# A ternary feed-forward laid between the steps of the next batch's attention

## The chip, the cores and the metric

The kernel runs on one NeuronCore of a Trainium2 chip. The metric is the device time of one execution in microseconds, the median of several runs. The profile is of one further execution. The engines are called by their short names: PE (TensorE, with PEld for its weight loads), DVE (VectorE), ACT (ScalarE), POOL (GpSimd) and SP (SyncE, which here only issues DMAs).

## The reference, cut to what matters

Eight sequences of 512 tokens and 128 features go through two transformer blocks with adaptive layer norm (shift, scale and gate come from a small conditioning vector). The first block has a one-head attention and a feed-forward with 4-bit quantization; nothing of it changes. The second block has an attention with 16 heads of 8 features, whose logits get a bias from "read" and "write" lines, and a feed-forward with ternary weights. It is this feed-forward that the change moves:

```
h  = layernorm(x) * (1 + scale) + shift
g  = silu(h @ w1.T * s1) * (h @ w2.T * s2)        # 128 -> 512
g  = gelu(g @ h1.T * t1)                          # 512 -> 512, ternary weights
g  = gelu(g @ h2.T * t2)                          # 512 -> 512
x  = x + gate * (g @ w3.T * s3)                   # 512 -> 128
```

The attention of a batch needs nothing of another batch, and so does the feed-forward of a batch: the second only needs the first of the same batch.

## The kernel before, in words

All of x stays in SBUF (`X`, 128 tokens by 32 tiles by 128). A batch is four tiles of 128 tokens. Everything is float32. The stages follow each other over all eight batches: first block's attention, first block's feed-forward, second block's attention (`attention1`), second block's feed-forward (the loop at the end).

The second attention is written out by hand (`tc.manual_schedule()`): the order of the calls is the order in each engine's queue. Its unit is a group of four heads of one batch, 32 groups in all. A group goes through three units of query tiles (`UNITS`: tiles 0 and 1 together, tile 2, tile 3) in four steps:

- `scores1` (L605): PE makes the scores of four heads in two pairs of PSUM banks (`quad`).
- `softmax1` (L622, L626, L629, L633): for each pair DVE adds the bias and takes the maximum, ACT takes the exponential.
- `turn1` (L646) and `turned1` (L652): PE transposes the probabilities of one head into a bank with tag "tp", of which there are two, and ACT copies them to SBUF.
- `values1` (L663): PE multiplies them with v and sums in a bank with tag "acc".
- `prep1` (L553 to L572) prepares queries and keys of the next group, and `lines1` (L584 to L594) its bias, into the same pairs of banks as the scores.
- `outcome1` (L676 to L699) takes a group's sums, divides and, after the fourth group of a batch, applies the output projection `py` and adds it to X. It is a generator: each `go(ended)` runs one more piece, between the steps of the next group.
- `front1` is a generator, too: norm, projections, lines and their norm for the next batch, one piece after each step (`go(front)`). Its logarithm and exponential at L528 and L531 stand on ACT.

The pools: eight PSUM banks are two "tp", two "acc" and four in the pairs. Tiles of queries' packs and keys' packs are kept twice (`packs["q", b % 2]`).

The last stage, the feed-forward, works on four batches at a time. It first makes w1 and w2 products (L794, L795), silu on 512 columns with the scale in the activation (L797) and the product (L798) for all four; then for each batch the two hidden layers (L814, 32 products, gelu L818 on 512 columns), the last layer (L825), the addition to X (L829) and the output DMA (L830). It has four PSUM banks ("mm") in turn besides the two "acc".

Of the kernel before, what the change touches and what calls it, by code (L numbers as in the profile page):

```python
# [10 lines left out]
F32 = mybir.dt.float32  # L11
# [6 lines left out]
P = 128  # L18
# [14 lines left out]
def kernel(ctx: ExitStack, tc: tile.TileContext, a: dict, out: bass.AP):  # L33
# [21 lines left out]
    def acc(name):  # L55
        return ps.tile([P, 512], F32, tag="acc", bufs=2, name=name)
# [338 lines left out]
    def lines_setup(pool):  # L395
# [48 lines left out]
        packs = {}  # L444
        for i in range(2):
            for name in ("q", "k"):
                pk = pool.tile(
                    [P, NT, H, 32], F32, tag=f"pack_{name}{i}", bufs=1, name=f"pack_{name}{i}"
                )
                nc.gpsimd.memset(pk, 0.0)  # L450
                packs[name, i] = pk
            pk = pool.tile([P, NT, H * VW + 32 - VW], F32, tag=f"pack_v{i}", bufs=1, name=f"pack_v{i}")
            nc.gpsimd.memset(pk, 1.0)
            packs["v", i] = pk
# [4 lines left out]

    def front1(pool, st, b, stats, bqs, packs):  # L460

        xb = X[:, b * NT : (b + 1) * NT, :]
        qp, kp, vp = (packs[name, b % 2] for name in "qkv")
# [18 lines left out]
        for t in range(NT):  # L482
            cur = hT[:, 1 + t * P : 1 + (t + 1) * P]
            pb = acc(f"pb_{b}_{t}")
# [20 lines left out]
        nc.gpsimd.tensor_sub(ln, ln, m2)  # L505
        for t in range(NT):
            cur = hT[:, 1 + t * P : 1 + (t + 1) * P]
            pa = acc(f"pa_{b}_{t}")
# [11 lines left out]
            if t == 1:  # L520
                nc.scalar.activation(m2, ln, AF.Square)
                ss = pool.tile([P, nln], F32, tag="ss", bufs=1, name=f"ss_{b}")
                nc.vector.tensor_reduce(ss, m2, AX.X, ALU.add)
                nc.vector.tensor_scalar_max(ss, ss, 1e-24)
            yield

        lg = pool.tile([P, nln], F32, tag="lg", bufs=1, name=f"lg_{b}")
        nc.scalar.activation(lg, ss, AF.Ln)  # L528
        rn = pool.tile([P, NT, 2, H], F32, tag="rn", bufs=1, name=f"rn_{b}")
        rv = rn.rearrange("p t w h -> p (t w h)")  # L530
        nc.scalar.activation(rv, lg, AF.Exp, scale=-0.5)  # L531
        nc.gpsimd.tensor_mul(lg, rv, rv)
        nc.gpsimd.tensor_mul(lg, lg, ss)
        nc.gpsimd.tensor_scalar(lg, lg, -0.5, 1.5, ALU.mult, ALU.add)
        nc.gpsimd.tensor_mul(rv, rv, lg)
        nc.gpsimd.tensor_mul(
            rn[:, :, 1, :], rn[:, :, 1, :], bsc.unsqueeze(1).to_broadcast([P, NT, H])
        )
        yield
        lnv = ln.rearrange("p (t w h) e -> p t w h e", t=NT, w=2)  # L540
        over = lambda w: rn[:, :, w, :].unsqueeze(3).to_broadcast([P, NT, H, NL])
        nc.gpsimd.tensor_mul(kp[:, :, :, 0:NL], lnv[:, :, 0], over(0))

        nc.gpsimd.tensor_mul(qp[:, :, :, 0:NL], lnv[:, :, 1, :, ::-1], over(1))
        yield

    def prep1(pool, st, b, g, packs, dk, dq):

        qp, kp = packs["q", b % 2], packs["k", b % 2]
# [7 lines left out]
        qT = pool.tile([P, T], F32, tag="qT", name=f"q1T_{b}_{g}")  # L557
        nc.scalar.copy(qT, pq)  # L558
        kT = pool.tile([P, T], F32, tag="kT", name=f"k1T_{b}_{g}")
# [15 lines left out]
    def lines1(pool, st, b, g, wdiag):  # L575
# [12 lines left out]
        st["bias", b, g] = bias = pool.tile([P, 4, NT, P], F32, tag="bias", name=f"bias_{b}_{g}")  # L588
# [61 lines left out]
    def turned1(st, b, g, u, j):  # L650
        pT, pt = st["pT", b, g, u, j]
        nc.scalar.copy(pT[:, : width1(u)], pt[:, : width1(u)])  # L652

    def values1(st, b, g, u, packs):

        if u == 0:
            st["po", b, g] = acc(f"po1_{b}_{g}")
# [12 lines left out]
    def outcome1(pool, st, b, g):  # L670
# [16 lines left out]
        if g == NG - 1:  # L687
# [5 lines left out]
            py = acc(f"py1_{b}")  # L693
# [6 lines left out]
            yield  # L700

    def attention1(pool, stats, dk, dq, wdiag, bqs, packs):
# [6 lines left out]
        go = lambda gen: next(gen, None)  # L709
        first = front1(pool, st, 0, stats, bqs, packs)  # L710
        for _ in first:
            pass
# [3 lines left out]
        for at, (b, g) in enumerate(groups):  # L716
            before = groups[at - 1] if at else None
            after = groups[at + 1] if at + 1 < len(groups) else None
            if g == 0:
                for _ in front:  # L720
                    pass
# [178 lines left out]
```

## Time and profile before

| | |
|---|---|
| median of 3 runs | 1687.32 us (1686.17 to 1698.59) |
| the profiled execution | 1685.65 us, span of its instructions 1683.6 us |
| mean granted clock of PE | 0.803 |
| PE busy | 1317.8 us, 78% |
| DVE, ACT, POOL busy | 753.9, 719.1 and 428.5 us |
| second attention | 485 to 1363 us |
| second feed-forward | 1363 us to the end |

The times count from the first instruction. A busy time of PE says how long matmuls were in flight; the granted clock says how fast they ran. The two have to be read together: the same matmul takes twice as long at clock 0.5. A window is a stretch of the span with the busy time of each engine in it. "Lxxx" is a line of the kernel before.

### The profile page before, as it was taken

The numbers are of one execution on the slowest core, as the hardware profiler recorded it, in microseconds if no ns is written. First come the engines' busy times: TensorE is split into PE (matmuls) and PEld (weight loads), VectorE is DVE, ScalarE is ACT, GpSimd is POOL, SyncE is SP. The second block draws the span as 40 slices with busy tenths as digits, with TensorE's granted clock in tenths as the row PEclk, the third lists the DMA queues.
The fourth block names the chain that finished last, engine by engine and source line by source line (L and its number), as shares of the span: only waits on it lengthen the run. The fifth ranks groups of instructions, "written<-read, shape, count | busy, mean of one in ns | idle before, by whom it ended". The sixth has DMA issues, their size and how long they took to land.

```text
span 1683.6 us, 22090 instructions
## 1 busy us (share of the span) xinstructions
PE 1317.8 (78%) x8644; PEld 814.0 (48%) x8644; DVE 753.9 (45%) x1545; ACT 719.1 (43%) x1440; POOL 428.5 (25%) x524
## 2 busy tenths in 40 slices
PE   4699343553448888988888888888888889999999
PEld 4355132433335555555555555555555544444444
DVE  3866854454425555455555555455545541003000
ACT  3243211221346555655555665555556552114111
POOL 0210322111254424343343244342432200000000
PEclk9799677676757777677687877777777789999999
DMA  6000000000000000000000000000000000000000
GB/s 178 1 1 0 1 0 0 0 0 0 0 0 1 1 1 1 1 1 1 1 1 1 2 1 1 1 1 1 1 1 2 1 1 1 13 7 7 7 7 12
DMA packets 14317, 10.96 MB, mean 7 GB/s; under 512 B 1862, under 2 KB 12678, under 8 KB 14214
## 3 DMA queue, kind: packets, MB, share of 16 engines
q1 hardware_dynamic: 12054, 8.02, 1.6%
q10 hardware_dynamic: 2160, 1.54, 0.3%
q8 instruction: 68, 1.11, 0.3%
q14 instruction: 35, 0.29, 0.1%
HBM read 7.46 MB, written 2.10 MB: 6 GB/s over the span
## 4 chain that ended last, share of the span: by engine, by line
PE 52%; ACT 13%; DVE 4%; POOL 2%; issue 2%; ACTq 0%; POOLq 0%; DVEq 0%
PE ph L814 13%; PE pr1T L646 11%; PE s L605 9%; ACT pr L633 7%; PE po L663 4%; ACT p1T L652 2%; PE pi L584 2%; PE ogT L159 2%; PE pg L794 2%; PE py L825 2%; PE pu L795 2%; DVE nm L629 1%; PE pa L509 1%; ACT k1T L560 1%; PE py L695 1%
## 5 line engine op out<-in xcount | busy, mean ns | idle before, releaser
L652 ACT COPY p1T<-pr1T 128x384 f32<-128x384 f32 (+1 forms) x384 | 195.7, 522 | 247.7 <-PE pr1T L646 247.4
L646 PE MATMUL pr1T<-ident,pr 128*128 128x128 f32 x1280 | 273.0, 369 | 23.7 <-ACT p1T L652 16.9
L605 PE MATMUL s<-kd,qd 14*128 14x128 f32 (+3 forms) x1024 | 196.5, 600 | 80.2 <-ACT pr L633 62.1
L646 PEld LDWEIGHTS pr1T<-ident,pr 128*128 128x128 f32 x1280 | 198.8, 187 | 110.8 <-ACT p1T L652 49.9
L633 ACT ACTIVATE pr<-s,nm 128x128 f32<-128x128 f32 (+3 forms) x512 | 234.6, 547 | 3.0 <-DVE nm L629 2.9
L814 PE MATMUL ph<-g,c_h 128*128 128x512 f32 x512 | 222.0, 592 | 0.0
L629 DVE TENSOR_REDUCE nm<-s 128x2 f32<-128x256 f32 (+3 forms) x256 | 205.0, 821 | 6.6
L814 PEld LDWEIGHTS ph<-g,c_h 128*128 128x128 f32 x512 | 96.4, 190 | 116.7 <-issue 116.7
L605 PEld LDWEIGHTS s<-kd,qd 14*128 14x128 f32 x1024 | 69.7, 224 | 154.4 <-ACT pr L633 69.9
L594 POOL TENSOR_SCALAR_AFFINE_SELECT bias<-bias 128x512 f32<-128x512 f32 x128 | 77.1, 635 | 208.2 <-DVE bias L590 208.2
L818 ACT ACTIVATE g<-ph,c_scl 128x512 f32<-128x512 f32 x64 | 44.0, 688 | 196.3 <-PE ph L814 196.3
L590 DVE TENSOR_TENSOR bias<-pi,wdiag 128x512 f32<-128x512 f32 x128 | 79.4, 683 | 104.3 <-PE pi L584 104.3
L357 PE MATMUL yTp<-ident,q_xn_y 128*88 128x128 f32 x128 | 27.5, 388 | 117.3 <-DVE q_xn_y L252 117.3
L829 DVE TENSOR_TENSOR X<-X,py 128x512 f32<-128x512 f32 x8 | 5.5, 687 | 243.3 <-PE py L825 243.3
L663 PE MATMUL po<-p1T,pack_v 128*32 128x128 f32 x2560 | 108.8, 317 | 0.0
L572 POOL TENSOR_TENSOR kd<-k1T,dk 128x128 f32<-128x128 f32 (+3 forms) x128 | 106.4, 861 | 0.0
L663 PEld LDWEIGHTS po<-p1T,pack_v 128*32 128x32 f32 x2560 | 77.0, 126 | 29.2 <-issue 27.1
L622 DVE TENSOR_TENSOR s<-s,bias 128x512 f32<-128x512 f32 x64 | 44.4, 694 | 85.0 <-PE s L605 85.0
L357 PEld LDWEIGHTS yTp<-ident,q_xn_y 128*88 128x88 f32 x128 | 21.6, 178 | 123.3 <-issue 121.9
L626 DVE TENSOR_TENSOR s<-s,bias 128x256 f32<-128x256 f32 x128 | 54.4, 425 | 58.0 <-PE s L605 53.1
L563 POOL TENSOR_TENSOR qd<-q1T,dq 128x512 f32<-128x512 f32 x32 | 40.4, 1263 | 124.4 <-ACT q1T L558 124.4
L807 POOL TENSOR_TENSOR w3b<-c_w,gs 128x512 f32<-128x512 f32 x8 | 10.1, 1268 | 241.5 <-PE py L825 241.5
(232 smaller groups left out, 1847.8 us busy)
## 6 DMA issues: line engine op xcount, KB each, us to landing
X<-in_x SPq DMA_DIRECT2D x8, 256.0 KB, 6.1
c_h<-in_h SPq DMA_DIRECT2D x2, 1024.0 KB, 10.3
out_x<-X SPq DMA_DIRECT2D x8, 256.0 KB, 2.3
c_wmod<-in_wmod ACTq DMA_DIRECT2D x2, 384.0 KB, 7.0
c_w<-in_w SPq DMA_DIRECT2D x3, 256.0 KB, 3.0
c_wqkv<-in_wqkv ACTq DMA_DIRECT2D x1, 192.0 KB, 7.1
c_bA<-in_bA ACTq DMA_DIRECT2D x1, 192.0 KB, 5.2
c_wA<-in_wA SPq DMA_DIRECT2D x1, 192.0 KB, 4.6
```

Source lines behind the costliest of these rows:

```text
L357: nc.tensor.transpose(pt[:CH0, c * P : (c + 1) * P], q[:, t, c, :], ident)
L572: nc.gpsimd.tensor_mul(kd[t], kT[:, : (t + 1) * P], dk[:, g, 384 - t * P :])
L590: nc.vector.tensor_mul(bias[:, j], pi[j // 2][:, j % 2].rearrange("p (t k) -> p t k", k=P), wdiag[:, 4 * g + j, :].unsqueeze(1).to_broadca ...
L594: nc.gpsimd.affine_select(out=bias[:, j], in_=bias[:, j], compare_op=ALU.is_ge, fill=NEG, base=0, pattern=[[0, NT], [-1, P]], channel_mult ...
L605: nc.tensor.matmul(s[j // 2][:, j % 2, at : at + (t + 1) * P], lhsT=qd[rk, t, :], rhs=kd[t][rk, :], start=True, stop=True,)
L626: nc.vector.tensor_add(diag, diag, bias[:, two, t, :])
L629: nc.vector.tensor_reduce(nm[:, n, two], s[:, :, at:end], AX.X, ALU.max, negate=True)
L633: nc.scalar.activation(pr[:, j, at:end], s[:, j % 2, at:end], AF.Exp, bias=nm[:, n, j : j + 1])
L646: nc.tensor.transpose(pt[:, c : c + P], pr[:, j, c : c + P], ident)
L652: nc.scalar.copy(pT[:, : width1(u)], pt[:, : width1(u)])
L663: nc.tensor.matmul(po[32 * j : 32 * j + 32, t * P : (t + 1) * P], lhsT=vp[:, k, h * VW : h * VW + 32], rhs=st["pT", b, g, u, j][0][:, at + ...
L814: nc.tensor.matmul(ph, lhsT=w[:, k, c * P : (c + 1) * P], rhs=src[:, k, :], start=(k == 0), stop=(k == NC1 - 1),)
```

## The change

The feed-forward of a batch is cut into 53 small units (`ffn1`), which `layer1` (the old `attention1`) takes from a list `todo`, one at a time, between the steps of the attention of the next batch. A unit is a pair of functions: the first issues PE's part, the second, issued later by `settle()`, the rest. `unit()` issues PE's part of the next unit, `fill(n)` settles and issues n units. Each of a group's four steps has one `unit()` in its middle and one `fill(2)` at its end. A batch's units are put on the list when its attention's result has been added to X, which is at the fourth step of the first group of the next batch. After the last group `fill(len(todo))` issues what is left.

The units of a batch: head (statistics and reciprocal root), norm, transposition; eight products with w1 and w2; silu and an empty unit; 16 products of the first hidden layer, gelu and an empty unit; the same for the second; four units of the last layer.

In the feed-forward, one PSUM bank with tag "ffn" holds each sum. DVE scales it into SBUF (`scaled`), and silu and gelu run once over 2048 columns (4 x 512) in place; the product with the second half is made by POOL in four pieces. After each of the three activations the table set of exponential and logarithm is loaded again (`tables()`).

Other edits that go with it:

- The sums of `values1` have one bank "po" of their own; the projections' `pb`, `pa` and `py` use the "tp" banks; the pool with "acc" is not kept in the second block.
- The packs of queries and keys, the tiles qT, kT and bias exist once, not twice.
- Of the four turned heads, the fourth is copied by DVE, not by ACT.
- In `front1` the lines' norm comes before the products with wA, its reciprocal root (`rsqrt`) follows the squares at once, and the table set loaded ahead of the stage is kept in the program's order.
- The statistics for the norm of the feed-forward are made for each batch in its head unit, with logarithm and exponential, not with a square root.

```
 def turned1(st, b, g, u, j):
     pT, pt = st["pT", b, g, u, j]
-    nc.scalar.copy(pT[:, : width1(u)], pt[:, : width1(u)])
+    if j < 3:
+        nc.scalar.copy(pT[:, : width1(u)], pt[:, : width1(u)])
+    else:
+        nc.vector.tensor_copy(pT[:, : width1(u)], pt[:, : width1(u)])
...
-            py = acc(f"py1_{b}")
+            py = tp(f"py1_{b}")
...
+    def ffn1(pool, b):
...
+        def head():
+            gs = pool.tile([P, D], F32, tag="gs", bufs=1, name=f"gs3_{b}")
+            nc.gpsimd.tensor_mul(gs, w3s, modb[1][:, b, 1, :])
+            st["wb"] = wb = pool.tile([P, NC1, D], F32, tag="wb", bufs=1, name=f"w3b_{b}")
+            nc.gpsimd.tensor_mul(wb, w3, rows(gs, NC1))
...
+            for t in range(NT):
+                nc.vector.bn_stats(sx[:, t, :], xb[:, t, :])
+                nc.vector.bn_aggr(mv[:, t, :], sx[:, t, :])
...
+            rsqrt(r, lg, v)
...
+        def bank(name):
+            st["bank"] = four.tile([P, 512], F32, tag="ffn", name=name)
+            return st["bank"]
...
+        def first(c, i):
+            if c == 0:
+                buf("ga"[i])
+            nc.tensor.matmul(
+                bank(f"pg1_{b}_{c}_{i}"), lhsT=(w1, w2)[i][:, c * P : (c + 1) * P], rhs=st["hT"],
+                start=True, stop=True,
+            )
+
+        def hidden(l, c, k):
+            ph = bank(f"ph{l}_{b}_{c}") if k == 0 else st["bank"]
+            nc.tensor.matmul(
+                ph, lhsT=(h1, h2)[l][:, k, c * P : (c + 1) * P], rhs=st["ga"[l]][:, k, :],
+                start=(k == 0), stop=(k == NC1 - 1),
+            )
+
+        def scaled(dst, c, i):
+            nc.vector.tensor_scalar_mul(st[dst][:, c, :], st["bank"], scl[:, i, c : c + 1])
+
+        def silu():
+            nc.scalar.activation(st["g"], st["g"], AF.Silu)
+            tables()
+            for c in range(NC1):
+                nc.gpsimd.tensor_mul(st["g"][:, c, :], st["g"][:, c, :], st["a"][:, c, :])
+
+        def gelu(k):
+            nc.scalar.activation(st[k], st[k], AF.Gelu)
+            tables()
...
+        units = [(none, head), (none, norm), (turn, none)]
+        for c in range(NC1):
+            for i in range(2):
+                units.append((lambda c=c, i=i: first(c, i), lambda c=c, i=i: scaled("ga"[i], c, i)))
+        units += [(none, silu), (none, none)]
+        for l in range(2):
+            for c in range(NC1):
+                for k in range(NC1):
+                    after = (lambda l=l, c=c: scaled("ag"[l], c, 2 + l)) if k == NC1 - 1 else none
+                    units.append((lambda l=l, c=c, k=k: hidden(l, c, k), after))
+            units += [(none, lambda l=l: gelu("ag"[l])), (none, none)]
+        for t in range(NT):
+            units.append((lambda t=t: last(t), end if t == NT - 1 else none))
+        return units
...
             softmax1(pool, st, b, g, 0, 0)
+            unit()
             softmax1(pool, st, b, g, 0, 1)
+            fill(2)
             go(front)
             for u in (1, 2, 3):
...
-                go(ended)
+                if go(ended) == "done":
+                    todo += ffn1(pool, before[0])
...
                 if u < 3:
                     softmax1(pool, st, *now, 0)
+                unit()
                 turn1(pool, st, *past, 2)
                 turned1(st, *past, 2)
                 turn1(pool, st, *past, 3)
                 if u < 3:
                     softmax1(pool, st, *now, 1)
                 turned1(st, *past, 3)
+                settle()
                 if u > 1:
                     values1(st, b, g, u - 2, packs)
+                fill(2)
                 go(front)
         values1(st, *groups[-1], 2, packs)
         for _ in outcome1(pool, st, *groups[-1]):
             pass
+        todo += ffn1(pool, B - 1)
+        fill(len(todo))
```

The whole loop of the old last stage (L775 to L830) is gone.

## The prediction

> **What bounds the kernel now.** I first read the slices: the attention of the second layer (485 to 1363 us) has a busy TensorE on a low clock, the feed-forward behind it (to the end) a full one. The windows, one batch of attention and four batches of feed-forward, give the numbers.
>
> ```profile
> PE   4699343553448888988888888888888889999999
> PEclk9799677676757777677687877777777789999999
> 846.30:955.50 109.20, 92.64 (x861) 59.68 (x860) 56.53 (x108) 63.02 (x136) 40.21 (x53) 0.78 0.00 1
> 1400.00:1522.00 122.00, 122.00 (x364) 60.54 (x364) 2.81 (x4) 23.14 (x33) 5.17 (x6) 1.00 0.02 7
> ```
>
> The columns of a window are its length, then busy us of PE, PEld, DVE, ACT and POOL, then the granted clock. A batch of attention takes 109.2 us; 321 us of feed-forward are 40.1 us a batch. Why attention is not PE at its peak shows in the timeline of a group's start and in windows of 3.4 us around it:
>
> ```profile
> 882.41 0.60 PE L553 MATMUL pkT<-ident,pack_k 128*128 128x128 f32 x4
> 883.67 1.36 ACT L633 ACTIVATE pr<-s,nm 128x128 f32<-128x128 f32 x4
> 885.13 0.92 PE L605 MATMUL s<-kd,qd 14*128 14x384 f32 x4 [1.47 <-ACT pr L633]
> 885.31 1.35 ACT L633 ACTIVATE pr<-s,nm 128x128 f32<-128x128 f32 x4 [0.28 <-DVE nm L629]
> 886.72 0.99 PE L605 MATMUL s<-kd,qd 14*128 14x384 f32 x4 [0.67 <-ACT pr L633]
> ...
> 880.30:883.70 3.40, 3.36 (x58) 2.21 (x54) 3.33 (x9) 1.65 (x4) 0.42 (x1) 1.00 0.00 0
> 883.70:887.10 3.40, 1.30 (x6) 0.63 (x8) 2.14 (x6) 2.68 (x9) 3.40 (x5) 1.00 0.02 5
> 887.10:890.50 3.40, 3.27 (x16) 2.34 (x13) 1.64 (x4) 0.49 (x2) 0.71 (x1) 0.55 0.00 0
> ```
>
> PE waits for the exponentials (1.47, then 0.67 us), and the next window has half the clock. I laid a grid of 3.41 us over the stage; the clock's changes fall on it, and it is half for 443 of 884 us. Of 44 full-clock windows with under 2.45 us of PE busy, 40 were followed by half clock; of 85 fuller ones, 7. None came back to full after a window under 3.1 us busy; of 111 above that, 48 did. So some 1.1 us of idle in one window costs several windows, 9.0 us on average, at half rate.
>
> **What is added.** A product of 128x512 is two matmuls. From these rows one takes 2 x 27.47/64 = 0.86 us.
>
> ```profile
> 1399.98 27.47 PE ph L814 x64
> 1428.98 2.90 PE py L825 x26
> L528 ACT ACT_TABLE_LOAD x8 | 10.3, 1283 | 0.1
> L247 ACT ACTIVATE q_big_y<-q_xn_y 128x1408 bf16<-128x1408 f32 x8 | 11.0, 1376 | 61.1 <-POOL q_xn_y L242 61.1
> ```
>
> A batch has 40 such products, 16 pairs of 128-column ones (32 x 0.111 us) and a transposition: 38.4 us of PE in 45 of its 53 units. A group of four heads offers 12 slots, a batch 48. The first unit can run late in group (1,0); from there to the end are 3 + 27 x 12 = 327 slots, so batches 0 to 5 and 9 units of batch 6 fit in, and 97 units follow after the last group.
>
> **One group at full clock.** I place the after-program's in-order queues on the group from 1286.29 us, which has no projection work of the next batch. Times count from its first scores; issue times are those of full-clock stretches (scores of the pair 0.87, values 1.0, eight transpositions 0.82, line products 1.1). PE is free at 2.70; three products last to 5.28, where the exponentials now let the next scores go at 5.1: no cost. The second half of them opens at 6.34 and ends at 7.0; transposition of o and two turns to 8.75 (the second turn waits for DVE at o's bank, 8.3), 1 product, two turns to 10.3, 2 products: next scores at 12.0 (11.5 in the trace). Third step: line products at 18.6 (17.8). Fourth: next group at 24.9 (24.2). So twelve products, 10.3 us of PE, cost 0.7 us as long as the clock is full, because they lie where PE waited and because they pay for the half clock that the trace has there. PE's work is 13.6 + 10.3 us of these 24.9. Four groups: 99.6.
>
> **What comes on top, per batch, at full clock.**
> - The one bank "ffn". After a finished sum of four, PE waits for matmul end to DVE 0.21, the scaling 0.70 (rows L273 0.749, L590 0.683) and 0.1 back, and longer where DVE has softmax in front. By slot of the group, the delay of the next step is 1.3, 0.6, 0, 2.2, 1.3, 0, 0.9, 1.0, 0, 0.8, 1.0, 0: 9.1 over 12. Sixteen of 53 units end a sum: 14.5 of 48, 11.0 us. Bounds 6 and 16. The largest, slot 4: the product ends at 9.6, but DVE has the second half's addition and maximum in front (to 11.1, rows L626 0.43 and L629 0.96) and a turn's copy (to 11.65); scaled at 12.35, next product 12.45 instead of 10.3.
> - Projections and outcome on PE: 16 short and 8 wide products and 12 transpositions, 5.7 us; the square root's chain in one step instead of two, 1.1. py now takes a "tp" bank: the second turn must wait until DVE has done four bias products (2.48) and the addition (0.68), 2.9 us. Sum 9.7.
> - Statistics, norm and square root of the feed-forward inside (DVE 1.8 + 1.1 us, ACT waiting for it): 2.5.
> - Silu and two gelus. 2048 columns are no row of this trace; from 512 (0.69) and 1408 columns (1.376) by slope 1.9 us; at least 1.4, at most four times 0.69 = 2.8. With a load before and one after, 1.9 + 2 x 1.28 = 4.5 us in which ACT, which copies every turned tile and does the exponentials, is closed. ACT is idle 1.7 to 2.0 us at three of the four steps, 4.2 at the last: 2.5 left each, and 2 us for the products on GpSimd (1.27 each) which the first hidden product awaits: 9.5. Bounds 5 and 15.
> - Eight units have no matmul: 2 back.
>
> Behind the load: two loads a batch at L528 and L531 (2.6 us) go, six come, and one of four copies of a turn moves from ACT to DVE (0.55 by L626 0.43 and L299 0.68); that is inside the walk. [...]
>
> Sum 99.6 + 11.0 + 9.7 + 2.5 + 9.5 - 2.0 = 130.3 us a batch at full clock, of which PE works 4 x 13.6 + 5.7 + 38.4 x 48/53 = 94.9: 73%, and idles 27% in lumps of one to three us.
>
> **The clock.** Lumps over about 1.1 us per batch: of the bank waits 4.7 (each slot comes 1.2 times a batch; 0.8 of it for the first, second and third largest, less for those near 1 us), 2.9 for the closed ACT, 0.9 for py, 1.6 for units without matmul, norm and square root: 10 in 130 us, one in 13. Half clock then lasts 9.0 us as now, or one window, 3.4; dense products refill it faster (1368 to 1372.1 us took one window), so I take one and a half, 5.1. Share at half: 5.1/(13 + 5.1) = 0.28. In a half-clock stretch PE makes 0.45 us of work per us (busy 0.9 of it), in a full one 0.73: 94.9/(0.72 x 0.73 + 0.28 x 0.45) = 145.6 us a batch. The same rule with the present stage's 60.1 us of work and share 0.5 gives its 109.2 at 0.65 for 0.73.
>
> [...] The windows above fell after 2.1 us of idle; I follow them.
>
> **The tail.** 97 units one behind the other. Per sum of four 3.43 + 1.0 us; 16 sums 71. Ten first products, 1.86 each at full clock; but they leave PE idle 1.0 of 1.9 us, so half clock, 2.7: 27. Twice silu, wait and POOL products 4, two gelus 2.1 each, last products 3.6, addition 0.9, and 7.5 of half clock after each pause: 41. Norm of batch 7: 7. Outcome of the last group 6. Together 152 us, where 1.83 batches cost 1.83 x 40.1 = 73 now. Bounds 130 and 165.
>
> **The sum.** Up to group (1,0)'s last step 628 us, less 5 for the loads and copies: 623. 27 groups are 6.75 batches: 983, less 6 for the last batch without projections. Tail 152. 623 + 977 + 152 = 1752; with the 2 us by which the profiled run's 1685.65 lies above its span of 1683.6, 1754. I round to 1750. The profiled run lies 0.1% under the median of 1687.32. To break even a batch may cost 135.5.
>
> **Rivals.**
> 1. The clock holds: the products fill the windows and the waits shrink to their lower bounds (bank 6, ACT 5). Then a batch is 130.3 - 5 - 4.5 = 121, to 128 with a share of 0.1 at half, and the tail 130 to 140: 623 + 6.75 x 121 - 6 + 135 = 1569 up to 1640; middle 1605. For it: 1.00 all through the dense stage, and three products that lie just in the gap that lowers the clock now. Against it: the one bank makes new gaps of 1.0 to 2.2 us. It decides from fewer than 4 falls of the clock per batch.
> 2. The clock is as bad as now, half of the time: 94.9/(0.5 x 0.73 + 0.5 x 0.45) = 161 us a batch, 623 + 1087 - 6 + 155 = 1859. For it: 9.0 us per fall today. Against: dense work that restores it.
> 3. The engines' load changes the bound: ACT gets 63.0 - 2.6 - 6.3 + 15 = 69, DVE 56.5 + 6 + 16 = 79 us a batch. Neither reaches 121, so this has no price of its own.
>
> **How the numbers follow.** Forecast (1690 to 1800) 0.54, of which 0.05 lies within 1%; the first rival 0.32, of which 0.03 reaches within 1%; the second 0.14. One per cent is about what a measurement of this kernel can tell from no change. Faster 0.29, same 0.08, slower 0.63. The range 1610 to 1840 leaves out the better half of the first rival and the worse half of the second.
>
> **What would show it.** Right: the last group of attention ends near 1600 us and a serial chain of 140 to 150 us follows with half-clock stretches in it; batches of 140 to 150 us; clock 0.83 to 0.88 in the stage; PE waiting for the scaling on DVE at the first product of a sum; turns that wait for ACT behind silu and gelu. Wrong: batches under 130 us with a clock above 0.93 (first rival), a wait of py's bank under 1 us, or a load of a table followed by idle time of its own.

## The result, and the profile after

The changed kernel takes 1699.77 us (median of 11 runs, 1692.54 to 1704.18) against 1689.24 us before in the same series: a ratio of 1.0055, with a 95% interval of 1.0032 to 1.0079. A clear slowdown of 3.6% was forecast; it is half a per cent. The profiled execution took 1692.54 us, the shortest of the 11; its span is 1690.8 us, and the mean granted clock rose from 0.803 to 0.836.

From the changed kernel's page the slices of the span, then three windows: the second and the sixth batch in the interleaved stage, and everything from the last batch's output projection to the end. Columns as before: length, busy us of PE, PEld, DVE, ACT and POOL, clock, DMA share, GB/s.

```profile
PE   3699343544448876888887688688979878877666
PEclk9799676676757788997998898799999978898969
620.15:759.75 139.60, 107.82 (x912) 63.17 (x908) 78.94 (x145) 70.03 (x133) 47.62 (x63) 0.91 0.00 1
1174.50:1302.97 128.47, 110.00 (x938) 65.68 (x934) 76.67 (x141) 66.01 (x130) 47.59 (x63) 0.93 0.01 3
1545.40:1690.80 145.40, 101.10 (x224) 43.99 (x224) 24.32 (x42) 28.02 (x21) 12.34 (x14) 0.81 0.01 4
```

The interleaved stage has a clock of mostly 8 and 9 (three slices have 7) where attention alone had 6 to 8, and the last tenth of the span is worse than the 9s that stood there: PE is busy 7 and 6 tenths. From one output projection `py` (L701) to the next, the batches take 139.6, 132.6, 143.4, 138.8, 128.5 and 132.9 us, 136.0 in the mean. Set beside the forecast (of the outcome's 6 us, some 3 lie ahead of the last `py`: ACT takes the group's sums at 1542.05, `py` starts at 1545.42):

| | forecast | profile after |
|---|---|---|
| up to the first `py` | 623 us | 620.2 us |
| from there to the last `py`: 6.75 batches with 6.17 batches of feed-forward inside | 980 us (977 and 3 of the outcome) | 925.2 us |
| a batch in it | 145.6 us | 136.0 us |
| falls of the clock per batch, length of one, share at half | 10, 5.1 us, 0.28 | 3.8, 7.6 us, 0.21 |
| from the last `py` to the end | 149 us (152 less these 3) | 145.4 us |

The start is right and the tail nearly so. The stage is 55 us shorter than forecast: six batches at 9.6 us less each are 58 of it. The row of falls shows a part of the reason.

### The profile page after: what moved, and what is told of

Its sections match the earlier page's. It is cut to its first block, busy times and chain, and to the rows that moved or that the text cites. A ratio compares the mean times of both kernels' runs of the same rounds, so it can differ in the third digit from the quotient of the medians.

```text
span 1690.8 us, 22087 instructions
## 1 busy us (share of the span) xinstructions
PE 1225.5 (72%) x8644; PEld 743.6 (44%) x8644; DVE 886.2 (52%) x1743; ACT 698.5 (41%) x1312; POOL 470.3 (28%) x586
## 4 chain that ended last, share of the span: by engine, by line
PE 43%; DVE 10%; ACT 9%; issue 7%; POOL 4%; ACTq 0%; POOLq 0%; DVEq 0%
PE ph L766 14%; PE pr1T L649 7%; PE s L608 6%; PE pg L759 4%; PE po L669 3%; ACT pr L636 3%; DVE nm L632 2%; PE py L787 2%; PE pi L585 2%; DVE ffn_g L772 2%; DVE ffn_a L772 2%; POOL kd L573 1%; PE ogT L159 1%; ACT p1T L656 1%; PE pa L531 1%
## 5 line engine op out<-in xcount | busy, mean ns | idle before, releaser
L656 ACT COPY p1T<-pr1T 128x384 f32<-128x384 f32 (+1 forms) x288 | 144.1, 516 | 283.2 <-PE pr1T L649 282.8
L649 PE MATMUL pr1T<-ident,pr 128*128 128x128 f32 x1280 | 217.4, 311 | 38.8 <-ACT p1T L656 20.9
L636 ACT ACTIVATE pr<-s,nm 128x128 f32<-128x128 f32 (+3 forms) x512 | 233.1, 546 | 11.0 <-DVE nm L632 10.8
L649 PEld LDWEIGHTS pr1T<-ident,pr 128*128 128x128 f32 x1280 | 167.0, 159 | 126.8 <-issue 48.4
L766 PE MATMUL ph<-ffn_g,c_h 128*128 128x512 f32 x256 | 137.1, 655 | 34.8 <-POOL ffn_g L778 17.9
L766 PE MATMUL ph<-ffn_a,c_h 128*128 128x512 f32 x256 | 134.7, 644 | 35.3 <-ACT ffn_a L781 16.9
L608 PE MATMUL s<-kd,qd 14*128 14x128 f32 (+3 forms) x1024 | 130.2, 524 | 19.4 <-ACT pr L636 10.9
L759 PE MATMUL pg<-hT,c_w 128*128 128x512 f32 x128 | 87.3, 770 | 42.4 <-DVE ffn_g L772 21.3
L593 DVE TENSOR_TENSOR bias<-pi,wdiag 128x512 f32<-128x512 f32 x128 | 79.4, 683 | 49.0 <-PE pi L585 49.0
L658 DVE COPY p1T<-pr1T 128x384 f32<-128x384 f32 (+1 forms) x96 | 57.4, 598 | 50.7 <-PE pr1T L649 50.7
L766 PEld LDWEIGHTS ph<-ffn_g,c_h 128*128 128x128 f32 x256 | 46.9, 207 | 84.0 <-DVE ffn_a L772 29.0
L766 PEld LDWEIGHTS ph<-ffn_a,c_h 128*128 128x128 f32 x256 | 45.9, 204 | 81.6 <-issue 30.9
```

What stands on the lines that cost most here:

```text
L593: nc.vector.tensor_mul(bias[:, j], pi[j // 2][:, j % 2].rearrange("p (t k) -> p t k", k=P), wdiag[:, 4 * g + j, :].unsqueeze(1).to_broadca ...
L608: nc.tensor.matmul(s[j // 2][:, j % 2, at : at + (t + 1) * P], lhsT=qd[rk, t, :], rhs=kd[t][rk, :], start=True, stop=True,)
L636: nc.scalar.activation(pr[:, j, at:end], s[:, j % 2, at:end], AF.Exp, bias=nm[:, n, j : j + 1])
L649: nc.tensor.transpose(pt[:, c : c + P], pr[:, j, c : c + P], ident)
L759: nc.tensor.matmul(bank(f"pg1_{b}_{c}_{i}"), lhsT=(w1, w2)[i][:, c * P : (c + 1) * P], rhs=st["hT"], start=True, stop=True,)
L766: nc.tensor.matmul(ph, lhsT=(h1, h2)[l][:, k, c * P : (c + 1) * P], rhs=st["ga"[l]][:, k, :], start=(k == 0), stop=(k == NC1 - 1),)
```

## The experiments

Every kernel is timed beside the kernel before; ratios are to that one, with 95% intervals (the two kernels of their own, which compute nothing of the reference, have one run each and no ratio). The kernels are the changed one with the edit shown. "Batch" is again the mean from one L701 to the next.

### What lowers the clock

Two pairs of windows on the 3.41 us grid of the changed kernel's trace (each of its 239 windows from 620 to 1436 us has a clock of 0.5 or 1.0, none one between) contradict the prediction's rule (under 2.45 us busy, the next window is at half). The first row of each pair is the window, the second the one behind it:

```profile
708.93:712.34 3.41, 2.67 (x14) 1.00 (x13) 1.05 (x2) 3.39 (x8) 3.41 (x5) 1.00 0.00 0
712.34:715.75 3.41, 1.88 (x9) 1.11 (x7) 2.90 (x6) 3.37 (x4) 0.25 (x1) 0.50 0.02 5
743.06:746.47 3.41, 1.75 (x9) 0.98 (x9) 3.08 (x6) 2.86 (x6) 0.53 (x1) 1.00 0.00 0
746.47:749.88 3.41, 3.41 (x18) 1.48 (x18) 0.07 (x1) 0.78 (x1) 0.00 (x0) 1.00 0.02 5
```

PE was busy 2.67 us and lost its clock; it was busy 1.75 us and kept it. The timeline of PE says what it did in the first window:

```profile
708.41 1.02 PE L766 MATMUL ph<-ffn_g,c_h 128*128 128x512 f32 x2
709.85 0.91 PE L608 MATMUL s<-kd,qd 14*128 14x384 f32 x4 [0.41 <-ACT pr L636]
711.09 0.92 PE L608 MATMUL s<-kd,qd 14*128 14x384 f32 x4 [0.33 <-ACT pr L636]
711.94 0.77 PE L159 MATMUL ogT<-ident,og 128*128 128x128 f32 x4
```

and in the second:

```profile
742.88 1.02 PE L766 MATMUL ph<-ffn_a,c_h 128*128 128x512 f32 x2
743.74 0.82 PE L649 MATMUL pr1T<-ident,pr 128*128 128x128 f32 x6
746.22 0.70 PE L766 MATMUL ph<-ffn_a,c_h 128*128 128x512 f32 x1 [1.66 <-DVE hT L480]
```

The first is filled with scores, whose weights have 14 rows (the first number of 14\*128); the second with products and transpositions of 128 rows, around 1.66 us of idle. So the theory to test was that rows in use count, not busy time. A kernel of its own measured kinds of matmuls by themselves: 14 dense products to warm up, then 16 turns of n units, each ended by a DVE copy that PE must wait for.

```
for i, (kind, n) in enumerate((k, n) for k in (dense, rows32, rows14, turn8) for n in (1, 2, 3)):
    ...
    for r in range(16):
        bank = psum.tile([P, 512], F32, tag="bank", name=f"bank_{i}_{r}")
        for _ in range(n):
            kind(bank)
        nc.vector.tensor_copy(y, bank)
```

> Measures the clock by itself: no transformer, only stages of matmuls. Each stage warms the clock with 14 dense 128x512 products and then runs 16 turns of n units of one kind into one bank, which DVE copies out, so that PE idles about 1.0 us after each turn. Kinds: product over 128 rows, over 32 rows, over 14 rows (as the scores), and eight transpositions; n = 1, 2, 3, that is PE busy about 46 to 57%, 63 to 70% and 72 to 77%. Theory 'busy time' (the forecast's): the share of busy time alone decides, under about 70% the clock falls: n = 1 and n = 2 at 0.5 for every kind, n = 3 at 1.0 for every kind. Theory 'weight': what counts is how much of the array works, so dense products hold 1.0 at n = 1 or 2 at least, and 14 rows and transpositions fall to 0.5 even at n = 2 or 3.

Windows of that kernel (855.03 us in one run; columns without ACT): dense products, n = 1; 32 rows, n = 1 and n = 3; 14 rows, n = 3; transpositions, n = 1.

```profile
29.00:58.00 29.00, 17.24 (x32) 4.65 (x31) 10.80 (x16) 0.00 (x0) 1.00 0.00 0
195.00:237.00 42.00, 30.25 (x32) 7.22 (x30) 10.57 (x16) 0.00 (x0) 0.52 0.00 0
337.00:432.00 95.00, 83.24 (x95) 27.70 (x93) 10.43 (x16) 0.00 (x0) 0.52 0.00 0
589.00:684.00 95.00, 83.25 (x96) 27.61 (x94) 10.54 (x16) 0.00 (x0) 0.52 0.00 0
699.00:727.00 28.00, 16.23 (x121) 12.68 (x120) 10.72 (x16) 0.00 (x0) 1.00 0.00 0
```

Products of 128 rows hold 1.00 at 59% busy (17.24 of 29.00), products of 32 or 14 rows lose it and then stay at half with PE 88% busy (83.24 and 83.25 of 95.00, clock 0.52). Transpositions, which I had put with the thin ones, hold 1.00 at 58% busy (16.23 of 28.00). The seven stages not shown go by kind alone, too: 1.00 for 128 rows and transpositions, 0.52 to 0.53 for 32 and 14 rows, whatever n is.

The same in the whole kernel: the products with w1, w2, h1 and h2 over 32 of the 128 rows, with the same instructions and waits.

```
-                bank(f"pg1_{b}_{c}_{i}"), lhsT=(w1, w2)[i][:, c * P : (c + 1) * P], rhs=st["hT"],
+                bank(f"pg1_{b}_{c}_{i}"), lhsT=(w1, w2)[i][0:32, c * P : (c + 1) * P], rhs=st["hT"][0:32, :],
...
-                ph, lhsT=(h1, h2)[l][:, k, c * P : (c + 1) * P], rhs=st["ga"[l]][:, k, :],
+                ph, lhsT=(h1, h2)[l][0:32, k, c * P : (c + 1) * P], rhs=st["ga"[l]][0:32, k, :],
```

> Changed kernel with the w1, w2, h1 and h2 products taken over 32 rows instead of 128 (three quarters of each sum are left out); as many matmuls, columns and waits. Theory 'busy time' or 'shorter waits': same time, 1690 to 1710 us, half-clock share of the stage 0.22 as now. Theory 'weight': the products no longer hold the clock; share at half 0.35 or more, time 1730 to 1800 us.

The six batches of the changed kernel, then those of this one:

```profile
620.15:1435.90 815.75, 662.64 (x5557) 396.89 (x5553) 462.58 (x840) 411.98 (x789) 283.85 (x376) 0.89 0.01 3
616.70:1691.10 1074.40, 963.41 (x5556) 539.24 (x5552) 466.57 (x840) 415.66 (x789) 283.21 (x376) 0.62 0.01 2
```

2036.63 us, ratio 1.2055 (1.1989 to 1.2120). As many matmuls (5556 for 5557) take 179.1 us a batch for 136.0, at a clock of 0.62 for 0.89, with PE busy 90% of the time. Less arithmetic, and 337 us more time; I had expected far less.

With these runs I counted every clock window of the traces anew. A matmul counts with 0.427 us for 512 columns (in the changed kernel's trace two such matmuls in a row start 0.853 us apart at half clock, twice this, and 0.429 at full clock) times its rows over 128; `po`'s count a quarter, because 24 of them in a row take 0.86 us and 32 take 1.08, so that each further one adds 27 ns, a quarter of the 107 ns of 128 columns. Call the sum row work; in a window it is the part of each matmul that lies there, spread evenly from its start to its end. What followed a window of the changed kernel's stage (620 to 1436 us): of 51 windows under 0.37 x 3.41 = 1.26 us of row work all 51 were followed by half clock, of 187 above it none. In the kernel before (484 to 1363 us) 124 of 124 and 3 of 132. The two windows above have 0.95 and 1.52 us.

That figure of 0.37 was fitted to the traces, and rows times columns of the weights fitted them as well. So one more kernel of its own took stages of 64 products in a row, with no wait at all, and different rows and columns.

```
    stages = [
        (64, 128), (52, 128), (44, 128), (128, 64), (128, 52), (128, 44), (128, 32),
        (88, 88), (72, 72), (128, 128),
    ]
    ...
            for _ in range(64):
                nc.tensor.matmul(bank[0:c, :], lhsT=h[0:r, 0, 0:c], rhs=mov[0:r, :], start=True, stop=True)
```

> A kernel of its own that computes nothing of the reference: ten stages, each of 14 products of 128 rows by 128 columns of weights and then 64 products, one directly behind the other without a wait, of fewer rows or columns (512 columns moving). From the windows of the runs so far: the clock of a 3.41 us window follows from the one before it. Each matmul is counted with the time its moving columns take at full clock (0.43 us for 512) times rows times columns of its weights over 128 times 128; where the sum is under some 0.37 of the window (1.3 us), the next one has half clock, else full. Theory, rows times columns: 64x128, 52x128, 128x64, 128x52, 88x88 and 128x128 (shares 0.50, 0.41, 0.50, 0.41, 0.47, 1.00) stay at clock 1.00 and their 64 products take 55 us; 44x128, 128x44, 128x32 and 72x72 (0.34, 0.34, 0.25, 0.32) fall to 0.5 after one window and take about 105 us. Rival, rows alone: all stages with 128 rows, 88x88 and 72x72 hold, 44x128 alone falls. Rival, the idle share alone as in the prediction: no stage falls, since TensorE never waits. Span about 900 us by the theory.

Windows inside the stages 52x128, 44x128, 128x32 and 72x72:

```profile
100.00:148.00 48.00, 48.00 (x113) 20.94 (x112) 0.00 (x0) 0.00 (x0) 1.00 0.00 0
168.00:264.00 96.00, 96.00 (x116) 37.61 (x115) 0.00 (x0) 0.00 (x0) 0.51 0.00 0
488.00:536.00 48.00, 48.00 (x114) 12.25 (x112) 0.00 (x0) 0.00 (x0) 1.00 0.00 0
622.00:670.00 48.00, 48.00 (x113) 16.01 (x112) 0.00 (x0) 0.00 (x0) 1.00 0.00 0
```

743.54 us in one run. Only 44 rows fell (share 0.34, clock 0.51), with PE busy all the time (96.00 of 96.00); 52 rows (0.41) held at 1.00, and so did 32 columns at 128 rows and 72 by 72: my theory of rows times columns is refuted, rows alone stands. By rows, with the limit at 0.37, 23 of 3996 windows in 14 profiles (both kernels and all twelve of these; from 485 us to the last `py`, in the kernel before to 1363 us, in the two kernels of their own nearly from end to end) are put on the wrong side, whichever clock the window itself had; in the kernel before these are 3 of 256 and in the changed one 1 of 309, where the best limit on busy time puts 78 and 48 wrong.

### What the dense products do to the attention

Three kernels take the change apart. In the first, units are held back until the attention has ended.

```
+        held = [False]
...
-            if todo:
+            if todo and held[0]:
...
+        held[0] = True
```

> Changed kernel with no unit issued inside the attention: all 8 x 53 units follow after the last group. Shows what the new attention costs alone and what a batch of units costs alone on one bank. Forecast's terms: first groups 5 us shorter than before, py's bank +2.9 and the reciprocal root +1.1 us a batch, fourth copy on DVE gains: attention 105 to 113 us a batch, clock about 0.75; units alone 74 to 80 us a batch (8 batches 590 to 640 us); total 1940 to 2000 us. If the copy on DVE matters more than thought: attention under 103 us.

Windows of that kernel: six batches of attention, and the units alone.

```profile
616.30:1226.50 610.20, 520.28 (x4936) 338.34 (x4932) 371.97 (x668) 329.95 (x723) 239.13 (x316) 0.81 0.01 1
1308.90:1969.50 660.60, 457.39 (x936) 185.95 (x936) 124.26 (x241) 116.90 (x96) 57.47 (x78) 0.77 0.01 3
```

1971.22 us, ratio 1.1659 (1.1624 to 1.1693). The attention takes 101.7 us a batch, the units alone 82.6: over twice the 40.1 of the former stage, and at a clock of 0.77. On the one bank and alone, the units lose to the former stage with its four banks; between the steps of the attention they add 31.7 us a batch (136.0 less the 104.3 of the next kernel).

The second goes back to the former feed-forward stage and keeps the new attention: interleaving alone is undone.

```
-                    todo += ffn1(pool, before[0])
+                    pass
...
-        todo += ffn1(pool, B - 1)
-        fill(len(todo))
...
+    (the loop of the kernel before, with its four "mm" banks and two "acc")
```

> The interleaving alone undone: the changed kernel's attention (one less ACT copy in four, one table set, packs and tiles once) without units, and then the former feed-forward stage with its four banks. From the run with all units last: 101.7 us a batch of attention against 109.2; the former stage 321 us: 1687 - 60 = 1627, 1615 to 1640 us. That would say that the interleaving itself loses about 70 us and the rest of the change gains 60. If the new attention only ran fast because of something after it: 1680 us.

```profile
616.80:1242.60 625.80, 531.87 (x4937) 345.19 (x4933) 378.78 (x717) 341.30 (x732) 239.63 (x316) 0.79 0.01 1
```

1645.32 us, ratio 0.9764 (0.9734 to 0.9794). A batch takes 104.3 us for the 109.2 before: the other edits of the change gain. (The same attention took 101.7 in the kernel above, so the gain is known to some 3 us a batch; what each edit has of it was not measured.) Its last `py` starts at 1325.6 us, its span is 1646.5. Against it the changed kernel loses 44 us of span, and the ledger is: first `py` 3 later, the stage between the first and the last `py` 925.2 for 708.8 us (216 more), the end 145.4 for 320.9 us (175 less).

The third adds to that kernel one dense product that nothing reads per `unit()`, twelve for a group.

```
-            if todo:
-                pe, rest = todo.pop(0)
-                pe()
-                late.append(rest)
+            held.append(0)
+            nc.tensor.matmul(
+                four.tile([P, 512], F32, tag="ffn", name=f"filler_{len(held)}"),
+                lhsT=h1[:, 0, 0:P], rhs=h2[:, 0, :], start=True, stop=True,
+            )
```

> The run with the changed attention and the former feed-forward stage, and in each of the 12 slots of a group one dense 128x512 product that nothing reads and that waits for no other engine (0.86 us at full clock, 41 us of PE a batch). Measures what PE's time alone costs between the steps. The forecast's walk: at full clock 0.7 us a group, so 99.6 us and 5.7 to 9.7 for projections: 106 to 110 us a batch at a clock of 0.97 or more, against 103 to 104 without; total 1645 + 6.75 x 2 to 7 and the first groups' slots: 1655 to 1705 us. If PE's time is simply added: 1645 + 8 x 41 = 1970 us.

```profile
617.00:1230.00 613.00, 588.18 (x4990) 326.40 (x4988) 342.64 (x650) 314.59 (x667) 218.80 (x290) 0.99 0.01 1
```

1718.45 us, ratio 1.0205 (1.0177 to 1.0233). 48 products a batch, 41 us of PE by themselves, make a batch 8.4 us longer (112.7 for 104.3), at a clock of 0.99 for 0.79. That is more than the 106 to 110 us expected, but far from the 41 us that plain addition would give. Mean row work of a window rises from 0.39 to 0.72 of its length.

### The terms of the sum

The bank: `scaled` is left out, and silu and gelu read constants instead.

```
         def scaled(dst, c, i):
-            nc.vector.tensor_scalar_mul(st[dst][:, c, :], st["bank"], scl[:, i, c : c + 1])
+            pass
```

> Changed kernel without the scaling of the sums by DVE (silu and gelu read a constant tile instead, the product takes another constant), so no product waits for the bank and DVE has 12 us a batch less. Forecast's term: 11 us a batch in 6.75 batches, and 1.0 us after each of 26 sums in the tail and its half clock: 1699 - 74 - 35 = 1590 us. By the waits in the changed kernel's trace (7.8 us a batch): 1699 - 53 - 35 = 1611 us. If these waits only take the place of waits for ACT: 1650 to 1665 us, the tail's part alone.

1585.55 us, ratio 0.9377 (0.9344 to 0.9411): 9.1 us off a batch (126.9), and 49 off the tail (1492.5 to the end at 1588.9 us). The edit also takes the scaling's work from DVE, so not all of this need be the bank.

The tables: Identity for silu and gelu, and no loads behind it.

```
-            nc.scalar.activation(st["g"], st["g"], AF.Silu)
-            tables()
+            nc.scalar.activation(st["g"], st["g"], AF.Identity)
```

> Changed kernel with Identity in the place of silu and gelu (same 2048 columns) and without the loads after them, so that one table set stays loaded through the stage: 6 loads of 1.283 us a batch go, nothing else. Forecast's term: an activation closes ACT for 4.5 us, 2.0 of them hidden; without loads 1.9, all hidden: 7.5 us a batch, 51 us in 6.75 batches, and little in the tail, where the loads lie under other waits: 1640 to 1655 us. Rival, the loads lie in ACT's idle time: 1685 to 1700 us.

1661.33 us, ratio 0.9855 (0.9833 to 0.9876): 4.3 us a batch (131.7), though the six loads of 1.28 us are 7.7, and Identity takes as long over 2048 columns (1.92 us) as the others. So part of the loads costs nothing; that it lies in idle time of ACT is the likely reason, and was not traced.

The product behind silu, on DVE instead of POOL.

```
-                nc.gpsimd.tensor_mul(st["g"][:, c, :], st["g"][:, c, :], st["a"][:, c, :])
+                nc.vector.tensor_mul(st["g"][:, c, :], st["g"][:, c, :], st["a"][:, c, :])
```

> Changed kernel with the four products after silu on DVE instead of POOL. Theory of a collision on POOL (its four products of 1.27 us hold back the lines' norm behind them, for whose squares ACT waits, and the first hidden products): per batch 2.4 us of PE waiting for POOL and about 2.9 of PE waiting for ACT go, and 4 x 0.6 us in each of two tails: 1650 to 1670 us. Rival, DVE's own 2.8 us a batch take their place: 1690 to 1705 us.

1692.87 us, ratio 1.0037 (1.0020 to 1.0054), not to be told from the changed kernel's 1.0055. The waits of PE in its stage (total, times, longest) show why:

```profile
PE pr1T L649 <- ACT p1T L656: 12.0, 13, 4.9
PE ph L766 <- DVE ffn_g L778: 10.8, 3, 5.9
```

The longest wait for ACT falls from 10.2 to 4.9 us, but the products now wait for DVE almost as long (10.8 us in 3 waits) as they did for POOL (14.6 in 4).

The tail: two banks in turn, from the pairs that the scores no longer need.

```
-            st["bank"] = four.tile([P, 512], F32, tag="ffn", name=name)
+            if tail:
+                tail.append(name)
+                i = len(tail) % 2
+                st["bank"] = four.tile([P, 2, 512], F32, tag=f"pair{i}", bufs=1, name=name)[:, 0, :]
+            else:
+                st["bank"] = four.tile([P, 512], F32, tag="ffn", name=name)
```

> Changed kernel in which the 97 units after the last group take two of the then free score banks in turn instead of the one bank. Forecast's tail: 26 waits of about 1.0 us, and the first products' half clock of 8 us, go: 1655 to 1670 us. (Without any scaling the tail came down from 145 to 96 us; here DVE still works.) If the tail is bound by its pauses: 1685 us or more.

```profile
1553.34:1674.30 120.96, 90.53 (x224) 44.28 (x224) 24.35 (x42) 28.00 (x21) 12.33 (x14) 0.85 0.01 4
```

1671.56 us, ratio 0.9907 (0.9878 to 0.9936). The tail takes 121 us for 145.4. A second bank takes away 24 us; no scaling at all took 49.

### Two versions that beat both kernels

Batches 0 to 5 go through the units, 6 and 7 through the former stage with its four banks.

```
-                if go(ended) == "done":
+                if go(ended) == "done" and before[0] < B - 2:
...
-        todo += ffn1(pool, B - 1)
         fill(len(todo))
...
+    (the loop of the kernel before, for the last two batches)
```

> Changed kernel in which the units of batches 0 to 5 run inside the attention as before and batches 6 and 7 go through the former feed-forward stage with its four banks, so that no unit follows on the one bank. 136 us a batch to group (7,3), nine units fewer there; then 6 us of outcome and 2 x 40.1 + 3 us instead of 146: 1700 - 60 = 1640 us, 1630 to 1650. That would put the loss of the tail, 60 to 70 us, against the gain of interleaving and meet the kernel without interleaving (1645).

```profile
620.10:1437.50 817.40, 663.42 (x5557) 397.01 (x5553) 462.52 (x848) 412.10 (x789) 283.96 (x376) 0.89 0.01 3
1533.90:1622.60 88.70, 80.66 (x240) 40.62 (x240) 12.33 (x28) 22.19 (x30) 3.31 (x4) 0.96 0.02 6
```

1624.26 us, ratio 0.9650 (0.9623 to 0.9677), the fastest kernel here that computes the whole. A batch is as in the changed kernel (136.2); what is left behind the last `py` takes 88.7 us at a clock of 0.96. The kernel with the new attention and nothing inside has a ratio of 0.9764 (0.9734 to 0.9794), so the interleaving by itself gains 1.2% once nothing is left over for one bank.

The same, with the scaling issued ahead of the second half's softmax and of the fourth copy, and an empty unit ahead of the turn of the norm.

```
-        units = [(none, head), (none, norm), (turn, none)]
+        units = [(none, head), (none, norm), (none, none), (turn, none)]
...
             unit()
+            settle()
             softmax1(pool, st, b, g, 0, 1)
...
                 turn1(pool, st, *past, 3)
+                settle()
                 if u < 3:
                     softmax1(pool, st, *now, 1)
                 turned1(st, *past, 3)
-                settle()
...
```

> As six_inside, with the scaling put on DVE ahead of the second half's softmax and of the fourth copy (so slot 1 and slot 4 no longer wait for them), and one empty unit between norm and transposition. By the forecast's table of slots the waits of slots 1, 4 and 7 (1.3, 2.2 and 0.9 us of 9.1 over 12) shrink by half: 2.7 us a batch; norm's wait, 23 us in six batches in the changed kernel's trace, goes: another 2 to 3 us a batch: six_inside less 30 us, about 1610. Rival, the softmax is late instead: no gain.

1643.84 us, ratio 0.9763 (0.9741 to 0.9786), slower than the kernel above. PE's waits in its stage:

```profile
PE ph L766 <- POOL ffn_g L778: 28.2, 6, 5.6
PE ph L766 <- ACT ffn_a L781: 18.2, 5, 4.3
PE py L787 <- ACT ffn_g L781: 16.5, 5, 4.3
PE pg L759 <- DVE ffn_g L772: 12.2, 14, 1.2
```

The waits for the norm are nearly gone (2.3 us for 22.5 in the kernel above) and those for the scaling are shorter, but the shifted units wait longer for POOL and the long activations: 63 us for 28.5. All waits together are even 8 us shorter (145 for 153), so they are not what makes the six batches 18 us longer. In windows at half clock PE is busy 180 us here and 135 above: more of its work fell into half clock. Which of the two edits moved it there was not separated.

## Why the prediction was wrong

**The clock: the step that failed.** The prediction took "some 1.1 us of idle in one window" as the cause of a fall, because in the trace of before the two go together: where PE idles there, it runs 14-row scores between its waits, so a window that is light by busy time is light by rows (of 43 full-clock windows under 2.45 us busy on the grid of the count, 39 are under 1.26 us of row work). The products of the feed-forward break that link: in the changed kernel's stage it is 20 of 38. Each product brings 0.86 us of row work, two thirds of the 1.26 under which windows were followed by half clock. So a bank wait beside dense products costs its own length and seldom a fall. Of the 10 falls a batch that the prediction gave, 3.8 came. It priced 4.7 of the 10 with the bank and 0.9 with `py`; with the scaling left out 19 falls remain in six batches, where the changed kernel has 23, so the bank has 0.7 a batch. Of the 23 windows ahead of the changed kernel's falls, ten have scores or line products (14 and 6 rows) in them.

Long gaps alone do not account for the falls either. The measured stage has nine gaps of PE over 3.41 us (up to 10.2), and eight of its 23 falls come with one; the other 15 have none, nor have 46 of the 47 falls in the kernel before, and the stage of 44 rows fell with no gap at all. The row work covers both kinds, since no row works in a gap.

**What the better clock is worth.** With the prediction's own formula and the measured share of 0.21 a batch comes to 94.9/(0.79 x 0.73 + 0.21 x 0.45) = 141.4 us: 4.2 of the 9.6 us. The other 5.4 lie in the formula's two rates. If its 94.9 us of work are shared out over the stage as PE's busy time times the clock is, PE did 0.79 us of work per us at full clock (forecast 0.73) and 0.37 at half clock (forecast 0.45), which gives the 136. At half clock PE was busy 0.76 of the time, not 0.9: the long waits fell there, while the formula had put all waits into full clock. The terms of the sum were checked with PE's waits of the changed kernel, 620 to 1436 us (six batches; total, times, longest):

```profile
PE pr1T L649 <- ACT p1T L656: 17.5, 13, 10.2
PE n3T L159 <- DVE n_f L734: 16.9, 7, 8.6
PE pg L759 <- DVE ffn_g L772: 15.7, 16, 1.5
PE ph L766 <- POOL ffn_g L778: 14.6, 4, 6.5
PE pg L759 <- DVE ffn_a L772: 12.1, 12, 1.7
PE ph L766 <- DVE ffn_a L772: 10.6, 11, 1.7
PE ph L766 <- DVE ffn_g L772: 8.5, 8, 1.7
...
PE n3T L159 <- DVE bias L593: 6.0, 1, 6.0
...
PE pr1T L649 <- DVE X L705: 0.3, 1, 0.3
```

- **The bank** (the four rows with L772): 46.9 us, 7.8 a batch, for 11.0 forecast. It lies within the bounds of 6 and 16; leaving out the scaling gained 9.1.
- **py's bank**: the turn was to wait 2.9 us a batch for the addition to X. The last row is that wait, 0.3 us in all six batches. A wait under 1 us was named as a sign of being wrong; this term was.
- **Silu and gelu**: the time of 2048 columns, forecast at 1.9 us, is 1.91 (below). Their closure was put at 9.5 us a batch. PE's waits for POOL's products, for the turned copies on ACT and for gelu (6.6 and 6.4 us at L766 and L787) are 45.1 us, 7.5 a batch.
- **The norm** of the feed-forward, forecast at 2.5 us a batch: the row with n_f, 16.9 us, and 6.0 more in one wait behind DVE's bias products (L593), 3.8 a batch.
- **The walk** of a group places twelve products; with the projections it is 99.6 + 9.7 = 109.3 us at full clock. The twelve dense products a group that nothing reads gave 112.7 at a clock of 0.99, without the 2.9 of `py` that are in the 109.3. So the walk was 3 to 6 us a batch too short.

As measured, these terms make 112.7 + 7.8 + 3.8 + 7.5 - 2.0 = 129.8 us, beside the forecast's 130.3 at full clock. That they agree is luck: the bank, `py` and the closures were priced too high, the walk and the norm too low.

**A collision that the walk did not have.** The one wait of 10.2 us shows in the timeline of the changed kernel:

```profile
657.22 1.28 ACT L775 ACT_TABLE_LOAD   x1
658.51 1.91 ACT L775 ACTIVATE ffn_g<-ffn_g 128x2048 f32<-128x2048 f32 x1
660.50 4.92 POOL L778 TENSOR_TENSOR ffn_g<-ffn_g,ffn_a 128x512 f32<-128x512 f32 x4 [13.23 <-ACT ffn_g L775]
665.38 1.80 POOL L512 TENSOR_TENSOR ln<-ln,m 128x768 f32<-128x768 f32 x1
667.22 0.84 ACT L513 ACTIVATE m<-ln 128x768 f32<-128x768 f32 x1 [5.49 <-POOL ln L512]
670.52 1.75 PE L649 MATMUL pr1T<-ident,pr 128*128 128x128 f32 x7 [10.19 <-ACT p1T L656]
```

The four products sit in POOL's queue ahead of the lines' norm (L512); ACT waits 5.49 us for that norm with the copies of the turned heads queued behind it, and PE waits for a copy. I had looked at each queue for itself. It came once in this length, and the kernel with the product on DVE shows that moving it alone gains nothing that can be measured. The load itself has no idle time behind it: it ends at 658.50 and silu starts at 658.51.

**The tail: nearly right, in part by luck.** First products one behind the other, at half clock, in the timeline of the changed kernel:

```profile
1617.34 2.08 PE L759 MATMUL pg<-hT,c_w 128*128 128x512 f32 x2 [0.84 <-DVE ffn_a L772]
1619.46 0.75 DVE L772 TENSOR_SCALAR ffn_g<-pg,c_scl 128x512 f32<-128x512 f32 x1 [2.17 <-PE pg L759]
```

The forecast said 2.7 us for each; it is 2.9 from one start to the next (1614.42, 1617.34, 1620.26). Half clock (0.50 from 1610 to 1625 us) is also what the row work gives: 0.86 us in 2.9 are 1.0 in a window, under the 1.26. But the parts do not fit as well as the sum: by the forecast's terms leaving out the scaling was to take 35 us off the tail and took 49, and a second bank was to take 34 and took 24.

**Where the gain of the interleaving went.** Of eight feed-forwards 327/53 = 6.17 are inside. They cost 6.17 x 40.1 = 247 us in the former stage and 216 inside: 31 won. The other 1.83 cost 73 us there and 145 in the tail: 72 lost. With the 3 of the start that is the 44 us of the ledger. The other edits of the attention gain 37 (1683.6 to 1646.5), so 7 us remain as a loss, the difference of the spans. Break-even was put at 135.5 us a batch, and 136.0 gave half a per cent more time: the sum over the stages holds. Neither its likeliest case nor the first rival came true: the falls, 3.8 a batch, are just under the 4 from which that rival was to decide, but the batch stayed 8 us above its upper end of 128. (That rival's upper end is 623 + 6.75 x 128 - 6 + 140 = 1621 us; the 1640 of the prediction does not follow from it.) That 1699.77 us still lies in the forecast's 1690 to 1800 says little: the chain of 145 us at the end and the waits for the scaling and for ACT came as forecast, but batches of 140 to 150 us, a stage clock of 0.83 to 0.88 and an attention that ends near 1600 us did not (136, 0.89 and 1542).

What stays open: why 23 of the 3996 windows do not follow the row count, whether the values that are multiplied matter (no run varied them), and what a batch would cost inside if ACT's closures were spread better than by the one shift tried here.

## What to carry to other kernels

Judge a low clock by how many rows of the array work in each window, not by PE's busy share (44 rows fell to 0.51 with PE busy all the time, 128 rows held 1.00 at 59% busy): dense full-row products are then worth placing between thin matmuls even where they leave PE idle beside them (41 us of them a batch brought the clock from 0.79 to 0.99 for 8.4 us). Before work is laid into slots, count what is left over after the last slot and give that rest the banks it had; here 1.83 batches on one bank ate more than twice what 6.17 batches had won. An activation over wide tiles closes its engine for whatever is queued behind it, and its consumer on another queue can close a second one: here 1.28 us of load and 1.91 of silu on ACT, then 4.92 of products on POOL, and PE waited 10.2 us.

## What was not expected of the hardware

- The clock went with the row work of the window before: 44 rows fell at 100% busy (0.51), 52 rows held (1.00), 128 rows held at 59% busy and transpositions at 58%; with 32 instead of 128 weight columns 128 rows held 1.00, too.
- One limit served both ways. Of the windows at half clock with over 0.37 of row work, 48 of 51 in the kernel before and 23 of 23 in the changed one were followed by full clock, of those under it none of 77 and none of 28: one window of 3.41 us above the limit was enough.
- Cutting the products to a quarter of their rows, at the same instructions, made the changed kernel 20% slower (2036.63 us for 1699.77).
